# Half of the probability transposes of a cross-attention block move from TensorE to the DMA queue, and the weight scales' diagonal is made one step earlier

## The chip, the cores and the metric

The kernel runs on one core of a Trainium2 chip. A core has five engines that run side by side, each through its own instruction queue in order: TensorE (PE in the profile; its weight loads are listed apart as PEld), VectorE (DVE), ScalarE (ACT), GpSimd (POOL) and SyncE (SP), which here only issues DMA transfers. TensorE reads the on-chip memory SBUF and writes the accumulation memory PSUM, which GpSimd and the DMA engines do not touch in this kernel. Engines wait for one another through semaphores.

The metric is the device time of one execution in microseconds (us). Before the change the median of 3 runs is 666.36 us (665.87 to 667.03).

## The reference

Two blocks follow each other on x, which has 2 batches of 2048 tokens with 512 features (4096 tokens in all):

```
x = x + tanh(g_xattn) * (softmax(q k^T / sqrt(32)) v) Wo^T + ...   # q from layernorm(x); k, v from 77 context rows; 16 heads of 32
x = x + tanh(g_ffn)   * qlinear(gelu(qlinear(layernorm(x), w1, b1)), w2, b2)   # 512 -> 2048 -> 512
```

`qlinear` rounds its input and its weight to integers of at most 127 in size, with one scale per tensor: the largest absolute value over the whole tensor, divided by 127. So the scale of w1 and w2, of the normalized x, and of the hidden layer each need a maximum over everything before anything can be rounded. Attention is computed in 32-bit floats throughout.

## The kernel before

**Tiling.** The 4096 tokens are cut into 8 blocks of 512 (index i in the code, NB = 8), each of four tiles of 128 tokens (t = 0 to 3). The 16 heads are cut into 4 groups of 4 heads (g). One attention step s (0 to 7 in each block) is one group and one half of the block: g = s // 2, and two 128-token tiles, u = 0 and u = 1. There are 64 steps in all.

**One step of attention.** `softmax(i, s)` (L286 to L323) does, for 256 tokens and 4 heads: eight score matmuls into PSUM (L295), the maximum over the 77 keys on DVE (L304), the subtraction on DVE into the tile `e`, 128 partitions (tokens) by 2 x 4 x 77 (L308), the exponential on ACT (L314), the sum and its reciprocal on DVE (L316, L318), and the multiplication by the reciprocal on POOL (L319). `transpose_a(i, s, u)` (L325) turns the result round, since the product with V needs the keys on the partitions: four PE transposes of 128x77 into one PSUM tile `pt` (L332), and one ACT copy into `aT` (L333). It is called for u = 0 and u = 1 in each step. After both steps of a group, `apply_v(i, g)` (L335) makes four matmuls `pc` of V and `aT` (L341), which ACT copies to `cT` (L349).

**What else happens in a step.** The main loop (L455 to L517) weaves other work between: `project_q` (pq, L276), `project_o` of the block before (po, L354), transposes of the next block's normalized x (ptx, L267), layernorm statistics, and the maxima for the quantization of the second layernorm (`norm2_stats`, `norm2_max`, L365 to L382). The scores run two steps ahead: in step s, PE does `apply_v` of the group before (even s only), the scores of step s + 2, the transposes of step s, and then one pq or po. So the probabilities of step s have somewhat less than two steps to become ready for PE, and those of an odd step s are wanted by pc at the beginning of step s + 1.

**Weights.** In the same loop `weight_step` (L411) finds the maximum of w1 (block i = 1) and w2 (i = 3), turns them into scales at step 0 of i = 2 and i = 4 with `scale_of` (L166), and rounds the weights in i = 2 and i = 4 (`quantize`, L198). `scale_of` takes a maximum per partition (`m`), multiplies it onto the identity (`diag`, L172), and has PE multiply a matrix of ones with this diagonal (`pg`, L174), so that all 128 maxima stand on each partition, where DVE takes the final maximum (L176). Weights are loaded by SP in pieces of 1 MB into the same rotating buffers (`big`) that hold x; a load waits until its buffer is free.

**What sets the order.** The order on PE is that of the program text (`manual_schedule`). On the other engines, SP among them, a planner places each instruction by its own estimate of when its operands and its buffer are ready; `issue_after` adds that one instruction stays behind another on its engine. Once placed, an engine's order is fixed, and an instruction that waits holds all behind it.

**Afterwards.** The first product of the feed-forward part starts at about 429 us; it takes x transposed by DMA as 16-bit data (L584: `xqT` from `xq`, 128x512 each, 28 times), sends most hidden tiles to DRAM and brings them back for the second product. The change does not touch this part beyond the names of two helpers.

Of the kernel before, what the change touches and what calls it, by code (L numbers as in the profile page):

```python
# [7 lines left out]

F32 = mybir.dt.float32
BF16 = mybir.dt.bfloat16  # L10
AF = mybir.ActivationFunctionType
ALU = mybir.AluOpType
AX = mybir.AxisListType
# [2 lines left out]
P = 128  # L16
D = 512
KC = D // P
HEADS = 16
DK = D // HEADS  # L20
NK = 77
HG = P // DK
NG = HEADS // HG
# [19 lines left out]
def tile_flamingo_gated_block(  # L43
# [20 lines left out]
    nc = tc.nc  # L64
    B = ctxT.shape[0]
# [20 lines left out]
    def kchunks(w):  # L86
        return w.rearrange("(kc p) n -> p kc n", p=P)
# [4 lines left out]
    awts = actx.enter_context(tc.tile_pool(name="awts", bufs=1))  # L92
    wq_sb = awts.tile([P, KC, D], F32, name="wq_sb")
    wo_sb = awts.tile([P, KC, D], F32, name="wo_sb")
    ctx_sb = awts.tile([P, B, KC, NK], F32, name="ctx_sb")
    kblk = [awts.tile([P, NG, RK], F32, name=f"kb{b}") for b in range(B)]
    vblk = [awts.tile([NK, D], F32, name=f"vb{b}") for b in range(B)]
    work = actx.enter_context(tc.tile_pool(name="work", bufs=2))
    bv_sb = work.tile([NK, D], F32, tag="cT", name="bv_sb", bufs=7)
    bq_sb = const.tile([P, KC], F32, name="bq_sb")  # L100
    bk_sb = const.tile([P, KC], F32, name="bk_sb")
    tg = const.tile([P, 2], F32, name="tg")
# [7 lines left out]
        engine.dma_start(dst[:, :, c], kchunks(src)[:, :, c])  # L110

    def load_ctx(engine, b):
        engine.dma_start(ctx_sb[:, b, :, :], kchunks(ctxT[b]))

    load_x(0, pieces=NT, engines=(nc.sync, nc.scalar))
    load_ctx(nc.scalar, 0)
# [34 lines left out]
    xmax = const.tile([P, NB - 1 + NT], F32, name="xmax")  # L151
    hmax = const.tile([P, NB * GT * 2 + 1], F32, name="hmax")
# [10 lines left out]
        nc.gpsimd.tensor_tensor(rstd, ve, mhalf[:, :n], ALU.pow)  # L163
        return last

    def scale_of(maxima, name, psum, tag):  # L166


        m = const.tile([P, 1], F32, name=f"m_{name}")
        nc.vector.tensor_reduce(m, maxima, AX.X, ALU.max)  # L170
        diag = small.tile([P, P], F32, tag="diag", name=f"diag_{name}", bufs=1)
        nc.vector.tensor_scalar(diag, ident, m, None, ALU.mult)  # L172
        pg = psum.tile([P, 512], F32, tag=tag, name=f"pg_{name}")
        nc.tensor.matmul(pg[:, :P], ones, diag, start=True, stop=True)  # L174
        g = const.tile([P, 1], F32, name=f"g_{name}")
        nc.vector.tensor_reduce(g, pg[:, :P], AX.X, ALU.max)  # L176
        s = const.tile([P, 1], F32, name=f"s_{name}")
        nc.vector.tensor_scalar(s, g, MIN_RANGE, 1.0 / QP, ALU.max, ALU.mult)
        inv = const.tile([P, 1], F32, name=f"inv_{name}")
        nc.vector.reciprocal(inv, s)  # L180
        return s, inv
# [25 lines left out]
    with actx:  # L207
# [3 lines left out]

        for kb in kblk:
            nc.gpsimd.memset(kb, 0.0)

        def project_k(b, g):

            pk = ps_p.tile([P, 512], F32, tag="pp", name=f"pk{b}_{g}")
            for kc in range(KC):
                nc.tensor.matmul(  # L219
                    pk[:, :NK],  # L220
                    wk_sb[:, kc, g * P : (g + 1) * P],
                    ctx_sb[:, b, kc, :],
                    start=(kc == 0),
                    stop=(kc == KC - 1),
                )
            for j in range(HG):
                r = slice(j * DK, (j + 1) * DK)
                dst = kblk[b][r, g, j % RT * NK : (j % RT + 1) * NK]
                bias = bk_sb[r, g : g + 1]
                if j % 2 or b == 0:  # L230
                    nc.scalar.activation(dst, pk[r, :NK], AF.Identity, bias=bias)
                else:
                    nc.vector.tensor_scalar(dst, pk[r, :NK], bias, None, ALU.add)

        def project_v(b):

            pv = ps_p.tile([P, 512], F32, tag="pp", name=f"pvv{b}")
            for kc in range(KC):
                nc.tensor.matmul(  # L239
                    pv[:NK, :],  # L240
                    ctx_sb[:, b, kc, :],
                    wv_sb[:, kc, :],
                    start=(kc == 0),
                    stop=(kc == KC - 1),
                )
            nc.vector.tensor_tensor(vblk[b], pv[:NK, :], bv_sb, ALU.add)

        ln, xnT, qT, aT, cT, es = {}, {}, {}, {}, {}, {}

        def norm(i):  # L250

# [34 lines left out]
        def softmax(i, s):  # L286
            g, half = divmod(s, 2)
            n = f"{i}_{s}"

            ps = ps_s.tile([P, NR, 512], F32, tag="ps", name=f"ps{n}")  # L290
            for u in range(2):
                t = 2 * half + u
                for q in range(NR):
                    r = slice(q * RT * DK, (q + 1) * RT * DK)
                    nc.tensor.matmul(  # L295
                        ps[:, q, u * RK : (u + 1) * RK],
                        qT[i, g][r, t * P : (t + 1) * P],
                        kblk[i // NBB][r, g, :],
                        start=True,
                        stop=True,  # L300
                    )
            mx = small.tile([P, NR, 2, RT], F32, tag="mx", name=f"mx{n}")
            sc = ps[:, :, : 2 * RK].rearrange("p q (u r k) -> p q u r k", u=2, r=RT)
            nc.vector.tensor_reduce(mx, sc, AX.X, ALU.max)  # L304
            e = work.tile([P, 2, GK], F32, tag="e", name=f"e{n}", bufs=3)
            e4 = e.rearrange("p u (j k) -> p u j k", j=HG)
            last = {}
            last["DVE"] = nc.vector.tensor_tensor(  # L308
                e.rearrange("p u (q r k) -> p q u r k", q=NR, r=RT),
                sc,  # L310
                mx[:, :, :, :, None].to_broadcast([P, NR, 2, RT, NK]),
                ALU.subtract,
            ).ins
            last["ACT"] = nc.scalar.activation(e, e, AF.Exp, scale=SCALE).ins  # L314
            sm = small.tile([P, 2, HG], F32, tag="sm", name=f"sm{n}")
            nc.vector.tensor_reduce(sm, e4, AX.X, ALU.add)  # L316
            rs = small.tile([P, 2, HG], F32, tag="rs", name=f"rs{n}")
            nc.vector.reciprocal(rs, sm)  # L318
            last["POOL"] = nc.gpsimd.tensor_tensor(  # L319
                e4, e4, rs[:, :, :, None].to_broadcast([P, 2, HG, NK]), ALU.mult  # L320
            ).ins
            es[i, s] = e4
            return last  # L323

        def transpose_a(i, s, u):  # L325
            g, half = divmod(s, 2)
            t = 2 * half + u
            if t == 0:
                aT[i, g] = work.tile([NK, HG, TB], F32, tag="aT", name=f"aT{i}_{g}", bufs=3)
            pt = ps_t.tile([P, KC, P], F32, tag="pt", name=f"pta{i}_{s}_{u}")  # L330
            for j in range(HG):
                nc.tensor.transpose(pt[:NK, j, :], es[i, s][:, u, j, :], ident)  # L332
            nc.scalar.copy(aT[i, g][:, :, t * P : (t + 1) * P], pt[:NK, :, :])  # L333

        def apply_v(i, g):  # L335
            pc = ps_p.tile([P, TB], F32, tag="pp", name=f"pc{i}_{g}")
# [47 lines left out]

        wraw, wmax = {}, {}

        def load_w(name, src, pieces):
            for j in pieces:  # L390
                wraw[name, j] = big(f"raw_{name}{j}")
                nc.sync.dma_start(wraw[name, j], kchunks(src(j)))
# [18 lines left out]
        def weight_step(i, s):  # L411
            j, odd = divmod(s, 2)
            if i == 1 and odd:
                weight_max("w1", j)
            if i in (2, 4) and s == 0:
                name = "w1" if i == 2 else "w2"
                s_w[name], inv_w[name] = scale_of(wmax[name], name, ps_p, "pp")
            if i == 2 and odd:
                quantize(w1q[:, :, j * TB : (j + 1) * TB], wraw["w1", j], inv_w["w1"])
            if i == 3 and odd:  # L420
                weight_max("w2", j)
                if j < 2:
                    load_w("w2", w2_piece, [j + 2])
                else:
                    load_w("w2", w2_piece, [j - 2])
            if i == 4 and odd:
                quantize(w2q[:, j * KC : (j + 1) * KC, :], wraw["w2", j], inv_w["w2"])
                if j < 2:
                    load_w("w2", w2_piece, [j + 2])
# [22 lines left out]
        softmax(0, 0)  # L452
        softmax(0, 1)
        project_q(0, 1)
        for i in range(NB):  # L455
            for s in range(2 * NG):
                g, odd = divmod(s, 2)
# [10 lines left out]
                    last = softmax(i + 1, s + 2 - 2 * NG)  # L468
                for u in range(2):
                    transpose_a(i, s, u)  # L470
                if i == 0 and s == 1:
                    project_v(0)
                if i == 0 and s == 2:


# [51 lines left out]
                    last = norm2_max(NB - 1, t - 1, t)  # L527
        with tc.issue_after(last):
            norm2_max(NB - 1, NT - 1, NT)
        s_x, inv_x = scale_of(xmax, "x", ps_p, "pp")  # L530
        xq0 = work.tile([P, NT, D], BF16, tag="xnT", name="xq0", bufs=1)
        for t in range(NT):
            v, vq = xs0[:, t, :], xq0[:, t, :]
# [97 lines left out]
                    stored[i, a] = hidden_dram.tile([P, GF, TB], F32, name=f"h{i}_{a}")  # L631
                    nc.sync.dma_start(stored[i, a], G)
    w1ctx.close()
    s_h, inv_h = scale_of(hmax, "h", ps_g, "pg")
    s2 = const.tile([P, 1], F32, name="s2")


# [113 lines left out]
```

## Time and profile before

One execution was profiled. It took 665.6 us, of which 663.8 us are the span that the profile covers; the rest lies around it.

| | before |
|---|---|
| median of 3 runs | 666.36 us |
| profiled execution, its span | 665.6 us, 663.8 us |
| granted TensorE clock, mean | 0.979 |
| steady attention (i = 1 to 7) | 57.5 to about 404 us |
| end of attention to first feed-forward matmul | about 404 to 429 us |
| first product, second product | 429 to 546 us, 546 to 664 us |
| probability transposes on PE (pta) | 512, in 64 steps |
| ACT copies of them (aT) | 128, 68.3 us, 582 ns each |
| multiplications on POOL (e) | 64, 78.7 us, 1230 ns each |

In the page a group of instructions is written as line, engine, operation, output and inputs, shapes, count, then busy time and mean length of one, and at last the idle time of the engine before them and what ended it. A matmul's length contains the depth of the pipeline (285 ns for a transpose), so that what it takes from PE is read from the distance to the next one. A line of the waits names the waiting engine and line, who ended the wait, then total, number and longest in us. In a timeline a line gives start, length, engine, source line, operation and, in brackets, the idle time before and who ended it.

### The profile page before, as it was taken

To read this page: it belongs to the slowest core of one execution; us is meant where nothing else is said; L and a number is where in the kernel's file an instruction comes from. 1 tells how busy PE (TensorE), PEld (TensorE's weight loads), DVE (VectorE), ACT (ScalarE), POOL (GpSimd) and SP (SyncE) were. 2 spreads that over 40 slices of the span, in tenths; PEclk is the share of its full clock that TensorE was granted. 3 is DMA by queue.
4 is the path that set the end of the run, shared out by engine and by line. 5 is a ranking of instruction groups with operands and counts; after the bars stand their busy time and mean duration, and the time that the engine had idled before them with its cause. 6 is when DMAs were issued, how large, how long until landed. Compare 5 with 4: busy or idle time off the path is not lost.

```text
span 663.8 us, 8218 instructions
## 1 busy us (share of the span) xinstructions
PE 630.0 (95%) x3048; PEld 320.7 (48%) x3048; DVE 517.9 (78%) x809; ACT 342.9 (52%) x479; POOL 206.2 (31%) x161
## 2 busy tenths in 40 slices
PE   5999999899999899999999999599999979999997
PEld 4565555455455455455554554244444434444443
DVE  3676687887997997986876767999889878887441
ACT  4455444244444344444444442188999879645430
POOL 2234333243333243333333332000000009996000
PEclk9999999799999899999999999799999998999999
DMA  9902100023131113100000000079999208789962
GB/s 280 377 22 88 39 1 0 1 70 121 64 120 72 64 71 120 64 0 1 1 0 1 1 17 1 0 255 329 303 309 345 77 0 326 274 324 357 335 206 79
DMA packets 44255, 84.90 MB, mean 128 GB/s; under 512 B 18795, under 2 KB 22891, under 8 KB 38584
## 3 DMA queue, kind: packets, MB, share of 16 engines
q1 hardware_dynamic: 43112, 83.70, 35.8%
q10 hardware_dynamic: 1104, 0.69, 0.3%
q8 instruction: 24, 0.39, 0.2%
q14 instruction: 15, 0.12, 0.1%
HBM read 49.25 MB, written 31.46 MB: 122 GB/s over the span
## 4 chain that ended last, share of the span: by engine, by line
PE 87%; DVE 10%; ACT 2%; DMA 1%; issue 1%; POOL 0%; ACTq 0%; DVEq 0%
PE pf L668 17%; PE ph L604 17%; PE po L354 15%; PE pq L276 14%; PE pta L332 9%; PE ps L295 6%; PE pc L341 4%; PE ptx L267 2%; DVE tm L376 1%; DVE xf L185 1%; DVE e L308 1%; PE pvv L239 1%; PE pk L219 1%; DVE mx L304 1%; DVE sm L316 1%; DVE max_w L397 1%
## 5 line engine op out<-in xcount | busy, mean ns | idle before, releaser
L319 POOL TENSOR_TENSOR e<-e,rs 128x616 f32<-128x616 f32 x64 | 78.7, 1230 | 231.2 <-DVE rs L318 173.4
L276 PE MATMUL pq<-xnT,wq_sb 128*128 128x512 f32 x256 | 117.3, 602 | 0.8 <-ACT xnT L268 0.8
L668 PE MATMUL pf<-w2q,hq 128*128 128x512 bf16 x512 | 113.6, 386 | 2.3 <-DVE hq L201 2.0
L354 PE MATMUL po<-wo_sb,cT 128*128 128x512 f32 x256 | 114.8, 593 | 0.0
L604 PE MATMUL ph<-xqT,w1q 128*128 128x512 bf16 x512 | 112.1, 382 | 0.7 <-DVE xqT L544 0.7
L333 ACT COPY aT<-pta 77x512 f32<-77x512 f32 x128 | 68.3, 582 | 77.0 <-PE pta L332 76.9
L611 ACT ACTIVATE G<-ph,b1s,s 128x512 f32<-128x512 f32 x128 | 99.5, 778 | 14.1 <-PE ph L604 3.3
L314 ACT ACTIVATE e<-e 128x616 f32<-128x616 f32 x64 | 45.9, 717 | 75.0 <-DVE e L308 73.4
L668 PEld LDWEIGHTS <-hq 128*128 128x128 bf16 x512 | 50.7, 99 | 64.9 <-issue 3.6
L621 DVE TENSOR_REDUCE hmax<-G 128x1 f32<-128x1024 f32 (+1 forms) x65 | 76.6, 1196 | 6.7 <-ACT G L611 6.7
L604 PEld LDWEIGHTS <-w1q 128*128 128x128 bf16 x512 | 50.3, 99 | 62.2 <-issue 1.9
L332 PE MATMUL pta<-ident,e 128*77 128x128 f32 x512 | 72.0, 285 | 0.1
L304 DVE TENSOR_REDUCE mx<-ps 128x8 f32<-128x616 f32 x64 | 50.3, 786 | 27.9 <-PE ps L295 27.4
L276 PEld LDWEIGHTS pq<-xnT,wq_sb 128*128 128x128 f32 x256 | 47.2, 194 | 48.7 <-issue 47.8
L316 DVE TENSOR_REDUCE sm<-e 128x8 f32<-128x616 f32 x64 | 50.6, 790 | 24.7 <-ACT e L314 24.5
L354 PEld LDWEIGHTS po<-wo_sb,cT 128*128 128x128 f32 x256 | 46.4, 190 | 48.2 <-issue 46.6
L332 PEld LDWEIGHTS pta<-ident,e 128*77 128x77 f32 x512 | 57.1, 150 | 11.8 <-issue 10.4
L661 ACT ACTIVATE Gb<-Gb,inv_h 128x2048 f32<-128x2048 f32 x22 | 43.7, 2000 | 36.5 <-DMA Gb<-h 35.5
L295 PEld LDWEIGHTS ps<-kb,qT 64*128 64x128 f32 x512 | 36.4, 188 | 44.9 <-ACT qT L284 22.8
L682 POOL TENSOR_TENSOR x<-x,b_sb 128x512 f32<-128x512 f32 x32 | 56.2, 1793 | 0.1
L308 DVE TENSOR_TENSOR e<-ps,mx 128x616 f32<-128x616 f32 x64 | 51.0, 797 | 2.6
L295 PE MATMUL ps<-kb,qT 64*128 64x154 f32 x512 | 51.3, 320 | 1.6 <-ACT qT L284 1.5
(89 smaller groups left out, 594.7 us busy)
## 6 DMA issues: line engine op xcount, KB each, us to landing
h<-G SPq DMA_DIRECT2D x22, 1024.0 KB, 5.7
Gb<-h SPq DMA_DIRECT2D x22, 1024.0 KB, 7.5
raw_w<-in_w2T SPq DMA_DIRECT2D x8, 1024.0 KB, 5.0
out_y<-x SPq DMA_DIRECT2D x32, 256.0 KB, 2.8
x<-in_x SPq DMA_DIRECT2D x7, 1024.0 KB, 5.3
raw_w<-in_w1T SPq DMA_DIRECT2D x4, 1024.0 KB, 11.7
wk_sb<-in_wkT SPq DMA_DIRECT2D x4, 256.0 KB, 4.9
wq_sb<-in_wqT SPq DMA_DIRECT2D x4, 256.0 KB, 6.1
```

The lines of the kernel that those rows point to most:

```text
L276: nc.tensor.matmul(pq, wq_sb[:, kc, g * P : (g + 1) * P], xnT[i][:, kc, :], start=(kc == 0), stop=(kc == KC - 1),)
L295: nc.tensor.matmul(ps[:, q, u * RK : (u + 1) * RK], qT[i, g][r, t * P : (t + 1) * P], kblk[i // NBB][r, g, :], start=True, stop=True,)
L308: last["DVE"] = nc.vector.tensor_tensor(e.rearrange("p u (q r k) -> p q u r k", q=NR, r=RT), sc, mx[:, :, :, :, None].to_broadcast([P, NR, ...
L316: nc.vector.tensor_reduce(sm, e4, AX.X, ALU.add)
L319: last["POOL"] = nc.gpsimd.tensor_tensor(e4, e4, rs[:, :, :, None].to_broadcast([P, 2, HG, NK]), ALU.mult).ins
L332: nc.tensor.transpose(pt[:NK, j, :], es[i, s][:, u, j, :], ident)
L333: nc.scalar.copy(aT[i, g][:, :, t * P : (t + 1) * P], pt[:NK, :, :])
L354: nc.tensor.matmul(po, cT[i, g][:, t * P : (t + 1) * P], wo_sb[:, g, :], start=(g == 0), stop=(g == NG - 1),)
L604: nc.tensor.matmul(ph, w1q[:, kc, fc * P : (fc + 1) * P], cur[:, kc, :], start=(kc == 0), stop=(kc == KC - 1),)
L611: nc.scalar.activation(G[:, 2 * v + u, :], ph, AF.Gelu, bias=b1s[:, fc : fc + 1], scale=s1,)
L621: nc.vector.tensor_reduce(hmax[:, k + u : k + u + 1], G[:, 2 * v + u : 2 * v + u + n, :], AX.XY, ALU.max, apply_absolute_value=True,)
L668: nc.tensor.matmul(po[t], hq[:, fc, t * P : (t + 1) * P], w2q[:, fc, :], start=(fc == 0), stop=(fc == FC - 1),)
```

## The change

For each step the second tile (u = 1) takes another way. After the multiplication on POOL, a second POOL instruction reads the 4 x 77 floats of each token as pairs of 16-bit words and writes low and high halves apart into a buffer `planes`, 128 x (2 halves x 4 heads x 128), of which two exist, used in turn and zeroed once. A DMA on SP's queue transposes each of its eight 128x128 blocks into `eT` (two buffers). `transpose_a` for u = 1 is then one ACT copy that reads both halves from `eT` and interleaves them again into floats in `aT`. For u = 0 nothing changes.

To make room, the context `ctx_sb` no longer has its own storage: its two batches take two of the seven slots of `cT`, which are not yet in use then. `project_v(0)` is moved from step 1 of the first block to ahead of the loop.

`scale_of` is cut in two: `diagonal_of` (maximum per partition, diagonal) and the rest. For w1 and w2 the diagonal is made at step 7 of i = 1 and 3, and the matmul stays at step 0 of i = 2 and 4. For x and the hidden layer both halves are still called together.

```diff
-    ctx_sb = awts.tile([P, B, KC, NK], F32, name="ctx_sb")
+    ctx_sb = [work.tile([P, KC, NK], F32, tag="cT", name=f"ctx{b}", bufs=7) for b in range(B)]
+    planes = [awts.tile([P, 2, HG, P], U16, name=f"planes{k}") for k in range(2)]
...
-    def scale_of(maxima, name, psum, tag):
+    def diagonal_of(maxima, name):
         m = const.tile([P, 1], F32, name=f"m_{name}")
         nc.vector.tensor_reduce(m, maxima, AX.X, ALU.max)
         diag = small.tile([P, P], F32, tag="diag", name=f"diag_{name}", bufs=1)
         nc.vector.tensor_scalar(diag, ident, m, None, ALU.mult)
+        return diag
+
+    def scale_of(diag, name, psum, tag):
         pg = psum.tile([P, 512], F32, tag=tag, name=f"pg_{name}")
         nc.tensor.matmul(pg[:, :P], ones, diag, start=True, stop=True)
...
         for kb in kblk:
             nc.gpsimd.memset(kb, 0.0)
+        for half in planes:
+            nc.gpsimd.memset(half, 0)
...
             es[i, s] = e4
+            p = planes[s % 2]
+            words = e4[:, 1, :, :].bitcast(U16).rearrange("p j (k h) -> p h j k", h=2)
+            nc.gpsimd.tensor_copy(p[:, :, :, :NK], words)
+            eT[i, s] = work.tile([P, 2, HG, P], U16, tag="eT", name=f"eT{n}", bufs=2)
+            nc.sync.dma_start_transpose(
+                eT[i, s].rearrange("p h j n -> p (h j) n"), p.rearrange("p h j k -> p (h j k)")
+            )
             return last
...
-            pt = ps_t.tile([P, KC, P], F32, tag="pt", name=f"pta{i}_{s}_{u}")
+            dst = aT[i, g][:, :, t * P : (t + 1) * P]
+            if u == 1:
+                nc.scalar.copy(
+                    dst.bitcast(U16).rearrange("p j (n h) -> p h j n", h=2), eT[i, s][:NK]
+                )
+                return
+            pt = ps_t.tile([P, KC, P], F32, tag="pt", name=f"pta{i}_{s}")
             for j in range(HG):
                 nc.tensor.transpose(pt[:NK, j, :], es[i, s][:, u, j, :], ident)
-            nc.scalar.copy(aT[i, g][:, :, t * P : (t + 1) * P], pt[:NK, :, :])
+            nc.scalar.copy(dst, pt[:NK, :, :])
...
             if i in (2, 4) and s == 0:
                 name = "w1" if i == 2 else "w2"
-                s_w[name], inv_w[name] = scale_of(wmax[name], name, ps_p, "pp")
+                s_w[name], inv_w[name] = scale_of(wdiag[name], name, ps_p, "pp")
...
+            if i in (1, 3) and s == 2 * NG - 1:
+                name = "w1" if i == 1 else "w2"
+                wdiag[name] = diagonal_of(wmax[name], name)
...
         project_q(0, 1)
+        project_v(0)
...
-                if i == 0 and s == 1:
-                    project_v(0)
```

More of the change, by code (lines that the diff above doesn't have):

```diff
@@ L10 @@
 BF16 = mybir.dt.bfloat16
+U16 = mybir.dt.uint16
 AF = mybir.ActivationFunctionType
@@ L112, in load_ctx @@
     def load_ctx(engine, b):
-        engine.dma_start(ctx_sb[:, b, :, :], kchunks(ctxT[b]))
+        engine.dma_start(ctx_sb[b], kchunks(ctxT[b]))
     load_x(0, pieces=NT, engines=(nc.sync, nc.scalar))
@@ L221, in project_k @@
                     wk_sb[:, kc, g * P : (g + 1) * P],
-                    ctx_sb[:, b, kc, :],
+                    ctx_sb[b][:, kc, :],
                     start=(kc == 0),
@@ L240, in project_v @@
                     pv[:NK, :],
-                    ctx_sb[:, b, kc, :],
+                    ctx_sb[b][:, kc, :],
                     wv_sb[:, kc, :],
@@ L246, in project_v @@
             nc.vector.tensor_tensor(vblk[b], pv[:NK, :], bv_sb, ALU.add)
-        ln, xnT, qT, aT, cT, es = {}, {}, {}, {}, {}, {}
+        ln, xnT, qT, aT, cT, es, eT = {}, {}, {}, {}, {}, {}, {}
         def norm(i):
@@ L382, in norm2_max @@
             ).ins
-        wraw, wmax = {}, {}
+        wraw, wmax, wdiag = {}, {}, {}
         def load_w(name, src, pieces):
@@ L529, in tile_flamingo_gated_block @@
             norm2_max(NB - 1, NT - 1, NT)
-        s_x, inv_x = scale_of(xmax, "x", ps_p, "pp")
+        s_x, inv_x = scale_of(diagonal_of(xmax, "x"), "x", ps_p, "pp")
         xq0 = work.tile([P, NT, D], BF16, tag="xnT", name="xq0", bufs=1)
@@ L633, in tile_flamingo_gated_block @@
     w1ctx.close()
-    s_h, inv_h = scale_of(hmax, "h", ps_g, "pg")
+    s_h, inv_h = scale_of(diagonal_of(hmax, "h"), "h", ps_g, "pg")
     s2 = const.tile([P, 1], F32, name="s2")
```

## The prediction

> **What bounds the kernel now.** I read the page's first part, then windows cut at the first score matmul of each 512-token block, then the waits, then a timeline of single steps. Columns of a window: length, busy time and instruction count of PE, PEld, DVE, ACT, POOL, then granted clock, DMA share, GB/s.
>
> ```profile
> PE 630.0 (95%) x3048; PEld 320.7 (48%) x3048; DVE 517.9 (78%) x809; ACT 342.9 (52%) x479; POOL 206.2 (31%) x161
> ...
> 57.50:105.60 48.10, 48.10 (x252) 25.73 (x248) 36.39 (x61) 22.34 (x39) 16.30 (x15) 1.00 0.13 44
> 105.60:159.50 53.90, 50.87 (x248) 27.51 (x244) 46.20 (x79) 21.39 (x36) 18.35 (x14) 0.94 0.12 40
> 159.50:206.80 47.30, 47.26 (x244) 25.14 (x240) 43.00 (x74) 20.85 (x36) 17.77 (x15) 1.00 0.24 90
> 206.80:259.20 52.40, 49.37 (x248) 26.65 (x244) 46.19 (x79) 21.39 (x36) 18.62 (x14) 0.97 0.21 81
> 259.20:306.50 47.30, 47.26 (x244) 25.15 (x240) 38.28 (x71) 21.06 (x36) 18.95 (x15) 1.00 0.13 45
> 306.50:353.80 47.30, 47.30 (x246) 25.22 (x242) 35.81 (x67) 21.09 (x36) 16.76 (x14) 1.00 0.00 1
> ```
>
> These are i = 1 to 6. Attention is bound by PE with no gap, except in i = 2 and i = 4, and DVE is close behind: 46.2 us of work in i = 2 and 4, 43.0 in i = 3. The exceptions are one wait each:
>
> ```profile
> PE pg_w L174 <- DVE rs L318: 6.1, 2, 3.0
> ...
> 122.30:125.30 3.00, 0.00 (x0) 0.03 (x1) 2.91 (x8) 0.72 (x1) 0.00 (x0) 0.95 0.01 3
> 125.30:134.00 8.70, 8.70 (x30) 5.13 (x30) 6.82 (x15) 1.78 (x3) 3.65 (x3) 0.63 0.00 0
> ```
>
> PE stands 3.0 us for the weight maximum's diagonal, then runs at clock 0.63: the two steps concerned span 18.0 us (117.0 to 135.0) where an ordinary pair takes 11.4. Excess 6.6 us in i = 2, and likewise 16.5 against 11.4, 5.1 us, in i = 4.
>
> The distance that the DMA route must fit in is seen in one odd step:
>
> ```profile
> 206.77 1.22 POOL L319 TENSOR_TENSOR e<-e,rs 128x616 f32<-128x616 f32 x1 [3.84 <-ACT qT L284]
> ...
> 212.72 0.87 PEld L332 LDWEIGHTS pta<-ident,e 128*77 128x77 f32 x8 [0.16 <-POOL e L319]
> ...
> 213.66 3.60 PE L276 MATMUL pq<-xnT,wq_sb 128*128 128x512 f32 x8
> ...
> 217.19 1.06 PE L341 MATMUL pc<-aT,vb 77*32 77x512 f32 x8
> ```
>
> The probabilities multiplied at 206.77 are ready at 207.99, PE transposes them at 212.72 (eight in 0.94 us, up to pq), and the product with V needs them at 217.19. From "ready" to pc is 9.2 us here. Over all odd steps of i = 1 to 6 I find 7.9 to 15.0 us, mostly 8.4 to 11; even steps have one step (over 5 us) more. The last step of all has only 2.8 us.
>
> [...] no one-input copy is in this trace, and the two-input multiply of 616 elements takes 1217 ns[...].
>
> **The change, part by part.**
>
> *PE transposes.* 4 of 8 leave each of 64 steps: half of 0.94 less the start, 0.45 us. 64 x 0.45 = 28.8 us at most, 3.6 per block.
>
> *Diagonal earlier.* m_w and diag_w (0.14 + 0.28 us of DVE) move one step ahead of the pg matmul, some 5 us. DVE is behind at that place (norm-2 maxima of the block before), but the diagonal now stands before the next scores, not behind them. PE's wait and slow clock should go: 6.6 and 5.1 us as far as PE is concerned. But then DVE bounds those blocks.
>
> *Blocks.* After = the larger of (PE without the excess, less 3.6) and (DVE work, plus about 1.8 us of waits for exp that DVE cannot fill, 5.7 us over i = 2 to 4). i = 1: 44.5 (-3.6). i = 2: PE 43.7, DVE 46.2 + 1.8 = 48.0 (-5.9). i = 3: DVE 43.0 + 1.8 = 44.8 (-2.5). i = 4: DVE 48.0 (-4.4). i = 5, 6, 7: PE (-3.6 each). i = 0: -3.0, since the first loads occupy the DMA engines until about 33 us, and the first two transposes queue behind them; project_v(0) moved forward fills PE's 1.3 us idle at 24.5. Sum -30.2.
>
> *Separation on GpSimd.* [...] POOL rises from 18 to 26 us of 44 per block: not a bound. Behind the copy stand the add of bo and rstd; the copy also waits for the plane's transpose of two steps before, long done. A busier POOL may slow DVE's tensor_scalar work (xf took 0.53 alone and 0.80 beside a multiply): inside my losses below.
>
> *DMA transpose.* The page's row:
>
> ```profile
> xqT<-xq SPq DMA_TRANSPOSE x28, 3.7
> ```
>
> That is four 128 x 128 blocks each: 1.19 us of SP and 2.4 us to landing when nothing else moves, 3.7 median beside stores, 6.5 at most. The new one has eight blocks. I add 1.2 us for the four more: SP 2.4, landing 3.6 to 3.7 (bounds 2.6, if the cost is all fixed, and 7.4, twice the median). Per block of 44 us SP issues 8 x 2.4 = 19 us, the DMA engines are busy about 8 x 1.2: neither binds.
>
> *Joining on ACT.* Two 77x512 copies at 582 ns become one and a 1024-element copy. ACT rows of 616 and 2048 elements (717 and 2000 ns) give 0.9 ns per element and 165 fixed: 1.08 us[...]. ACT goes from 21 to 25 us per block. Not a bound, but the join waits for a DMA with exp, qT and cT queued behind it.
>
> *Chain.* Copy 1.1, SP and landing 3.8, join 1.2: 6.1 us after "ready". Available at odd steps: the 8.4 to 11 above less three half transposes, 1.35, so 7 to 9.6; the tightest is 7.9 - 1.35 = 6.6. It just fits, everywhere but at the end: the last step has 2.8 - 0.4 = 2.4, so PE stands 3.7 us before the last pc, with nothing to cover it, and perhaps a slow clock after: **+3.9**.
>
> *Loads on the same queue.* From 60 us on 14 loads of 1 MB share SP's ring, each occupying the engines about 3 us. A transpose issued behind one comes 2 to 3 us late; at odd steps 1 of these is slack. 14 x 0.7 (chance to be hit) x 0.5 (odd) x 1.3 is about **+6**. SP is in order too: a load waiting for its buffer (up to 71.8 us for x, on w1q) would stop the transposes behind it. The planner places a load when its buffer falls free by its own estimate, so a mismatch of 1 to 2 us per load is what I expect; with ACT's joins standing a little before exp I put **+4** (0 to 15) for both.
>
> Moving ctx_sb to the cT slots and two memsets on an idle POOL: nothing.
>
> Sum: -30.2 + 3.9 + 6 + 4 = -16.3. The profiled execution (665.6 us, span 663.8) goes to about 649; the median shown is 0.8 above that execution, so **650 us**.
>
> **Rivals.**
>
> *The DMA route is too long (slower).* From the score matmul to pc PE has about 15.2 us of work left per odd step (two short steps of 4.7, one long of 5.7), and the chain takes 7.5 (to "ready") + 1.1 + landing + 1.3. If landing is D, every pair of steps stalls by half of D - 5.3, because the stall before also counts. At D = 7.4 that is 1.05 us x 30 pairs, 31 us, in place of the +6: 675. It turns from gain to loss near D = 6.5. For it: 6.5 has been seen, with half the size. Against: those stood beside 1 MB stores, and attention moves 1 to 90 GB/s.
>
> *ACT stands in joins (slower).* If the planner reckons a shorter DMA than the chip's, each join holds exp and DVE starves. In i = 2 to 4 DVE has no room, so each us per step costs 24; at 1 us per step 650 + 24 = 674, deciding from 0.7 us. For it: ACT is in order and the planner doesn't know real landings. Against: exp has slack against its next use elsewhere.
>
> *All hides (faster).* The loads and joins cost nothing: -26, so 640; with DVE's work spread over neighbouring blocks 636.
>
> *The change does nothing:* excluded by PE's lost work, unless stalls eat it; I count 3 in 100 for landing within 0.2%, about what measurement can tell from no change.
>
> **How the numbers follow.** Likeliest 0.56 (own range 641 to 661), all hides 0.12, DMA too long 0.16, ACT in joins 0.16, of which the two slower ones end under the old time 3 times in 100 and within 0.2% 3 times. Faster 0.71, same 0.03, slower 0.26. The range takes in the rivals' centres: 637 to 677.
>
> **What would show it.** Right: no wait of pg on DVE; half the pta count; blocks of 44 to 45 us with PE full in i = 1, 5, 6, DVE near full in i = 2 to 4; transposes landing in 3 to 5 us; a gap of 3 to 5 us before the last pc. Wrong: pc waiting for ACT aT in most pairs (DMA too long), ACT's idle put down to the DMA with DVE waiting for exp (joins), SP waiting for a load's buffer while probabilities lie ready, or a separation copy over 2 us.

## The result, and the profile after

The changed kernel is slower. Its median is 719.89 us (718.20 to 721.02, 4 runs) beside 666.12 us (664.34 to 667.03, 4 runs) for the kernel before: a ratio of 1.0813, 95% interval 1.0783 to 1.0844. The prediction was 650 us. The profiled execution took 718.2 us with a span of 716.4 us, 52.6 us longer than the span before.

First the page's part on engines, then its groups of instructions; both of the kernel after. Its line numbers differ a little from those of before: the score matmul `ps` is L303, the exponential L322, the multiplication on POOL L327, the separation L335, the DMA transpose L337, the join L349, the remaining copy behind PE's transposes L356, the product `pc` L364.

```profile
PE 627.1 (88%) x2792; PEld 303.4 (42%) x2792; DVE 520.8 (73%) x809; ACT 385.1 (54%) x479; POOL 257.1 (36%) x227
...
L349 ACT COPY aT<-eT 77x1024 uint16<-77x1024 uint16 x64 | 85.6, 1338 | 108.3 <-DMA eT<-planes 108.3
...
L335 POOL COPY planes<-e 128x616 uint16<-128x616 uint16 x64 | 51.6, 806 | 2.0
```

PE has 256 instructions fewer and fell from 95% to 88% of the span. The group that stands out is the join: each takes 1338 ns, and ahead of the 64 of them ACT stood idle for 108.3 us in all, until the landing of a DMA.

Windows of the kernel after, cut at the first score matmul of each block, i = 1 to 6 (length, then busy time and count of PE, PEld, DVE, ACT, POOL, granted clock, DMA share, GB/s):

```profile
64.30:116.60 52.30, 46.97 (x222) 23.39 (x218) 36.49 (x61) 28.27 (x42) 22.48 (x22) 0.97 0.35 81
116.60:171.20 54.60, 44.64 (x212) 21.98 (x212) 46.60 (x79) 26.54 (x37) 26.20 (x22) 0.98 0.38 90
171.20:226.20 55.00, 48.29 (x210) 23.91 (x210) 44.26 (x72) 26.50 (x37) 23.52 (x22) 0.93 0.46 115
226.20:282.50 56.30, 47.87 (x212) 23.68 (x212) 46.59 (x79) 26.67 (x37) 26.19 (x22) 0.93 0.42 113
282.50:337.60 55.10, 48.93 (x208) 23.84 (x208) 38.26 (x69) 26.25 (x37) 23.14 (x22) 0.91 0.28 63
337.60:393.20 55.60, 49.36 (x208) 24.76 (x208) 36.41 (x67) 26.40 (x37) 21.73 (x22) 0.88 0.20 38
```

No engine fills its block: in i = 5 and 6 PE is busy 49 of 55 us, and part of that is its slower clock (0.91 and 0.88, 1.00 before). Before, these blocks took 47.3 us with PE full. The weights' blocks i = 2 and 4 no longer stand out; all blocks from i = 2 on take 54.6 to 59.0 us. So the loss is spread over all blocks: the eight grew by about 49 us together, from 0.8 us in i = 2, where the earlier diagonal gains, to 9.7 in i = 7. What lies between them and the first feed-forward product grew by 3.4.

The waits of the kernel after (engine and line, who ended the wait, total, number, longest):

```profile
ACT aT L349 <- DMA eT<-planes: 108.3, 53, 5.4
PEld ps L303 <- ACT qT L292: 56.2, 24, 6.1
DVE sm L324 <- ACT e L322: 54.2, 33, 4.6
PE ps L303 <- ACT qT L292: 34.6, 17, 5.2
PEld pc L364 <- ACT aT L349: 9.2, 2, 5.9
PE pc L364 <- ACT aT L349: 8.2, 2, 5.6
```

Three of these were far smaller before:

```profile
DVE sm L316 <- ACT e L314: 24.5, 35, 0.8
PEld ps L295 <- ACT qT L284: 22.8, 25, 2.2
PE ps L295 <- ACT qT L284: 1.5, 2, 1.3
```

The product that uses the joined data waits only twice, for 8.2 us. What waits is unrelated to it: DVE's sum for an exponential, and PE's scores for queries. Both are made on ACT, where they can stand behind a join. A timeline of the kernel after shows one such case (start, length, engine, line, operation, and in brackets the idle time before and who ended it; lines of other work left out):

```profile
309.72 0.70 POOL L335 COPY planes<-e 128x616 uint16<-128x616 uint16 x1
...
311.53 0.79 DVE L316 TENSOR_TENSOR e<-ps,mx 128x616 f32<-128x616 f32 x1
...
313.56 1.34 ACT L349 COPY aT<-eT 77x1024 uint16<-77x1024 uint16 x1 [3.68 <-DMA eT<-planes]
314.77 0.70 ACT L322 ACTIVATE e<-e 128x616 f32<-128x616 f32 x1
...
315.51 0.80 DVE L324 TENSOR_REDUCE sm<-e 128x8 f32<-128x616 f32 x1 [1.14 <-ACT e L322]
...
318.25 1.07 PE L364 MATMUL pc<-aT,vb 77*32 77x512 f32 x8
...
319.21 0.72 ACT L322 ACTIVATE e<-e 128x616 f32<-128x616 f32 x1 [1.97 <-DVE mean L162]
...
319.84 0.67 ACT L292 ACTIVATE qT<-pq,bq_sb 128x512 f32<-128x512 f32 x1
...
320.56 0.80 PE L303 MATMUL ps<-kb,qT 64*128 64x154 f32 x8 [1.24 <-ACT qT L292]
```

DVE has the scores of two steps on subtracted at 312.32. ACT could take their exponential then, but the join is ahead of it in ACT's order and waits for its transfer until 313.56. The exponential starts at 314.77, 2.45 us late, while the product that needs this join runs only at 318.25. The delay runs on from there: DVE stands 1.14 us for this exponential, so its next subtraction ends only at 319.10 (not shown) and the next exponential starts at 319.21. Behind that one, in ACT's order, stands the copy of queries whose projection was done at about 317.45 (not shown); it starts at 319.84, and PE's scores that read it start after 1.24 us of idling. In the whole kernel PE idles 34.6 us for queries, 1.5 before. ACT kept its order here: the exponential's operand was ready at 312.32, and nothing passed the join that waited until 313.56.

### The profile page after: what moved, and what is told of

It reads as the page before. It is cut to its first block, busy times and chain, and to the rows that moved or that the text cites. A ratio compares the mean times of both kernels' runs of the same rounds, so it can differ in the third digit from the quotient of the medians.

```text
span 716.4 us, 8015 instructions
## 1 busy us (share of the span) xinstructions
PE 627.1 (88%) x2792; PEld 303.4 (42%) x2792; DVE 520.8 (73%) x809; ACT 385.1 (54%) x479; POOL 257.1 (36%) x227
## 3 DMA queue, kind: packets, MB, share of 16 engines
q1 hardware_dynamic: 110696, 100.48, 47.2%
## 4 chain that ended last, share of the span: by engine, by line
PE 46%; DVE 22%; DMA 12%; POOL 7%; ACT 6%; issue 6%; SPq 0%; POOLq 0%; DVEq 0%; ACTq 0%
PE pf L693 16%; PE ph L629 16%; DMA eT<-planes 11%; PE po L377 8%; DVE sm L324 3%; POOL planes L335 3%; DVE e L316 3%; DVE mx L312 3%; ACT aT L349 2%; POOL x L279 2%; ACT e L322 2%; PE ps L303 2%; DVE x L384 2%; DVE xf L191 2%; POOL e L327 2%
## 5 line engine op out<-in xcount | busy, mean ns | idle before, releaser
L327 POOL TENSOR_TENSOR e<-e,rs 128x616 f32<-128x616 f32 x64 | 78.7, 1230 | 237.2 <-DVE rs L326 149.3
L349 ACT COPY aT<-eT 77x1024 uint16<-77x1024 uint16 x64 | 85.6, 1338 | 108.3 <-DMA eT<-planes 108.3
L377 PE MATMUL po<-wo_sb,cT 128*128 128x512 f32 x256 | 127.4, 646 | 0.0
L303 PE MATMUL ps<-kb,qT 64*128 64x154 f32 x512 | 55.7, 341 | 34.7 <-ACT qT L292 34.6
L377 PEld LDWEIGHTS po<-wo_sb,cT 128*128 128x128 f32 x256 | 52.1, 214 | 56.8 <-issue 54.9
L303 PEld LDWEIGHTS ps<-kb,qT 64*128 64x128 f32 x512 | 39.8, 203 | 79.7 <-ACT qT L292 56.2
L322 ACT ACTIVATE e<-e 128x616 f32<-128x616 f32 x64 | 45.7, 714 | 47.8 <-DVE e L316 39.2
L284 PEld LDWEIGHTS pq<-xnT,wq_sb 128*128 128x128 f32 x256 | 47.2, 195 | 48.8 <-issue 47.7
L686 ACT ACTIVATE Gb<-Gb,inv_h 128x2048 f32<-128x2048 f32 x22 | 43.7, 2000 | 33.9 <-DMA Gb<-h 33.9
L356 ACT COPY aT<-pta 77x512 f32<-77x512 f32 x64 | 36.9, 577 | 46.5 <-PE pta L355 46.4
L335 POOL COPY planes<-e 128x616 uint16<-128x616 uint16 x64 | 51.6, 806 | 2.0
```

The lines of the kernel that those rows point to most:

```text
L284: nc.tensor.matmul(pq, wq_sb[:, kc, g * P : (g + 1) * P], xnT[i][:, kc, :], start=(kc == 0), stop=(kc == KC - 1),)
L303: nc.tensor.matmul(ps[:, q, u * RK : (u + 1) * RK], qT[i, g][r, t * P : (t + 1) * P], kblk[i // NBB][r, g, :], start=True, stop=True,)
L327: last["POOL"] = nc.gpsimd.tensor_tensor(e4, e4, rs[:, :, :, None].to_broadcast([P, 2, HG, NK]), ALU.mult).ins
L335: nc.gpsimd.tensor_copy(p[:, :, :, :NK], words)
L349: nc.scalar.copy(dst.bitcast(U16).rearrange("p j (n h) -> p h j n", h=2), eT[i, s][:NK])
L377: nc.tensor.matmul(po, cT[i, g][:, t * P : (t + 1) * P], wo_sb[:, g, :], start=(g == 0), stop=(g == NG - 1),)
```

## The experiments

**Theory A** (from the profile above): the loss is the wait for a DMA in ACT's order. The route itself is cheap and early enough for `pc`; but the planner set every join ahead of the exponential of two steps on, and some directly ahead of a query copy, so the DMA's latency enters the chain that feeds the next scores. **Rivals**: the extra work itself (longer join, separation copy, DMA traffic); the transfer too late for `pc`; the changed place of the diagonal. The first four kernels tell these apart.

**The join without the wait.** It does the same work on constants, so the second tile's probabilities are left out of the result.

```diff
             if u == 1:
+                halves = ones[:NK].bitcast(U16).rearrange("p (h n) -> p h n", h=2)
+                halves = halves[:, :, None, :].to_broadcast([NK, 2, HG, P])
                 nc.scalar.copy(
-                    dst.bitcast(U16).rearrange("p j (n h) -> p h j n", h=2), eT[i, s][:NK]
+                    dst.bitcast(U16).rearrange("p j (n h) -> p h j n", h=2), halves
```

> The join is kept on ACT with its size and place in the step, but it reads a constant tile of ones in place of the transposed halves, so that it waits for no DMA (the second tile's probabilities are then not the true ones). Separation and DMA transposes still run. Theory A (ACT stands in joins that the planner put ahead of exp and qT, waiting for the DMA): all of the loss and most of the hoped gain come back, 645 to 660 us, and the waits of DVE for exp and of PE for qT shrink to the old size. Theory B (POOL, SP and DMA work in itself slows DVE or delays the probabilities, whoever reads them): stays above 700. Theory C (the join's length, 1.34 us in place of 0.58, overloads ACT): stays above 690.

Measured: 648.24 us (one run), span 646.5. All instructions are there, the joins keep their length and their places ahead of the exponentials, and 71.6 us are gone. Of the difference in span, 69.9 us, PE's busy time is 23.0 (627.1 against 604.1 for the same work, at a mean granted clock of 0.942 against 0.976) and its idle time 46.9. The joins of this kernel, and two of its waits:

```profile
L351 ACT COPY aT<-ones 77x1024 uint16<-77x1024 uint16 x64 | 83.5, 1337 | 0.1
...
DVE sm L324 <- ACT e L322: 27.0, 27, 1.7
PE ps L303 <- ACT qT L292: 4.9, 4, 1.7
```

**The join behind the exponential of two steps on.**

```diff
-                for u in range(2):
-                    transpose_a(i, s, u)
+                transpose_a(i, s, 0)
+                with tc.issue_after(last["ACT"]):
+                    transpose_a(i, s, 1)
```

> Only the order on ACT changes: each join is tied behind the exponential of the scores made in the same step; data, DMA and waits are those of the change. Theory A (order on ACT): exp is no longer held, DVE's wait for exp falls from 54 to about 25 us, and the time comes down to 650 to 680. Theory B2 (the chain from separation to join is too long for the two steps there are, whatever the order): stays at 705 to 725, with the wait moved to pc for aT.

Measured: 673.82 us (667.93 to 675.92, 4 runs), ratio to before 1.0101 (1.0052 to 1.0151). The order alone takes 46 us off the changed kernel, with the real transfer in place. It also moves the wait, as these waits of this kernel show:

```profile
PEld pc L364 <- ACT aT L349: 40.2, 22, 4.8
DVE sm L324 <- ACT e L322: 24.4, 29, 1.4
PE pc L364 <- ACT aT L349: 22.9, 18, 4.0
...
ACT aT L349 <- DMA eT<-planes: 9.5, 6, 2.9
```

ACT hardly waits any more and DVE's waits are those of before; now PE waits for late joins.

**The extra work without its use.** PE's transposes and both ACT copies stay; separation, DMA and the earlier diagonal are added, and nothing reads `eT`.

```diff
-            if u == 1:
-                nc.scalar.copy(
-                    dst.bitcast(U16).rearrange("p j (n h) -> p h j n", h=2), eT[i, s][:NK]
-                )
-                return
```

> All eight PE transposes and both ACT copies of before are kept, and separation on POOL and the DMA transpose run beside them with nobody reading the result; the diagonal is early as in the change. Theory A: the side work costs nearly nothing, 655 to 668 us (the early diagonal gains up to 10). Theory B (side work itself): 690 or more, near the changed kernel.

**The earlier diagonal alone**, on the kernel before, with `scale_of` cut in two as in the change (not shown):

```diff
+            if i in (1, 3) and s == 2 * NG - 1:
+                name = "w1" if i == 1 else "w2"
+                wdiag[name] = diagonal_of(wmax[name], name)
```

> The kernel before with only the diagonal of w1 and w2 a step earlier. My prediction's term: PE's two waits of 3.0 us and the slow clock after them go, 6 to 11 us, so 655 to 661 us. A rival: DVE is behind at that place anyway and PE waits for it at the next scores, 664 to 667.

Measured: 658.83 us with the side work (one run), and 656.79 us with the diagonal alone (656.34 to 656.94, 4 runs; ratio 0.9874, 0.9858 to 0.9889). The diagonal is worth 8.3 us (i = 2 fell from 53.8 to 48.4 us, i = 4 from 52.4 to 48.4), and all the side work costs about 2. Together with the kernel above, which has the longer joins, this puts the rivals of extra work and of the diagonal out.

**The wait alone.** This adds to the side-work kernel one ACT copy of a single column of `eT` per step. Nothing uses it, and the planner places it.

```diff
+            if u == 1:
+                peek = small.tile([NK, 1], U16, tag="peek", name=f"peek{i}_{s}")
+                nc.scalar.copy(peek, eT[i, s][:NK, 0, 0, :1])
```

> The side-work kernel (all PE transposes and both ACT copies as before, separation and DMA beside them, early diagonal; 658.8 us) plus one ACT copy of a single column of the transposed halves per step, placed by the planner. It adds no length to speak of (64 copies of some 0.2 us, 13 us of an engine half idle) and nobody uses it: all that it adds is ACT's wait for the DMA. Theory A: the wait alone brings most of the loss back, 690 to 725. If the wait is harmless: 659 to 664.

Measured: 706.57 us (701.71 to 709.53, 4 runs), ratio 1.0635 (1.0601 to 1.0668). Its group and its waits:

```profile
L354 ACT COPY peek<-eT 77x1 uint16<-77x1 uint16 x64 | 12.4, 194 | 145.4 <-DMA eT<-planes 145.3
```

```profile
DVE sm L324 <- ACT e L322: 63.4, 41, 4.1
PEld ps L303 <- ACT qT L292: 45.5, 26, 4.2
```

Copies that are busy for 12.4 us together cost 48 us, with the same two victims as in the changed kernel. No product depends on them. That settles theory A's core: the wait in the order is enough for a loss of this size. What makes up the rest of the 71.6 was not separated.

**The join on GpSimd** (`nc.scalar.copy` becomes `nc.gpsimd.tensor_copy`):

> The join runs on POOL in place of ACT, with the order left to the planner; the rest as in the change. Theory A (what counts is who stands behind the waiting join): on POOL there stand the next multiply, which needs 5 us anyway, so that the waits of DVE for exp and of PE for qT go back to the old size and the time falls to 655 to 680. Theory B2 (chain too long): stays near 700 to 720, with pc waiting for aT.

Measured: 721.03 us (720.41 to 723.78, 4 runs), ratio 1.0842 (1.0814 to 1.0870). This kernel's waits:

```profile
POOL aT L349 <- DMA eT<-planes: 109.3, 46, 4.6
PEld pc L364 <- POOL aT L349: 35.2, 15, 6.3
```

The time expected under theory A (655 to 680) was missed. DVE's waits for exponentials did fall to their old size (22.0 us), but the same wait now stands on the engine that also holds the next multiplication: PE idled 23.3 us for late joins and 10.6 for late probabilities. Taking the join off ACT freed ACT and helped nothing. By itself this kernel would fit the rival of a transfer too late for `pc` as well.

**Repairs that missed.** Five kernels tried to give the route more time. In "separate first", the separation copy must come ahead of the bias additions on POOL:

```diff
-            nc.gpsimd.tensor_copy(p[:, :, :, :NK], words)
+            last["POOL"] = nc.gpsimd.tensor_copy(p[:, :, :, :NK], words).ins
```

> The addition of bo on POOL is tied behind the separation copy (in the change it often stands between multiply and copy, 1.27 us); all else as in the change. Theory A (joins stand ahead of exp and qT on ACT and wait there): the DMA is up to 1.3 us earlier where the addition stood in between, about half of the steps, so ACT's wait for the DMA falls by 20 to 40 us and the time by 10 to 30, to 690 to 710. Theory B2 (chain too long): about the same number. It sizes this part of the chain.

In "product later", `pc` of groups 0 to 2 moves from the start of the even step into the odd step after it, ahead of the query projection, some 5 us later:

```diff
-                if not odd and s > 0:
-                    apply_v(i, g - 1)
-                elif not odd and i > 0:
+                if not odd and s == 0 and i > 0:
                     apply_v(i - 1, NG - 1)
...
+                if odd and s > 1:
+                    apply_v(i, g - 1)
```

> The product with V of groups 0 to 2 moves from the beginning of the even step to the odd step after it, some 5 us later in PE's order; the order on ACT is left to the planner. Theory A: pc was not what stood, exp and qT behind the joins were, so little is won: 705 to 720. Theory B2 (the chain is too long for the time up to pc): the slack cures it, 650 to 670.

With the planner's order of ACT, these measured 712.73 and 716.03 us (one run each): a few us, with ACT's wait still 98.8 and 111.8. The first fell short of what was expected. The second was expected at 650 to 670 if the transfer were too late for `pc`, so that rival is out as the cause. Both together, and the join behind the exponential:

> Three edits together: the product with V later, the join behind the exponential of its step, separation ahead of the addition of bo. Theory A says that the 25 us still missing between the join behind exp (673.8) and the join without a wait (648.2) are pc waiting for a join that now comes late; with 5 us more up to pc most of it should come back: 648 to 660, and pc's wait for aT falls from 40 to under 15 us. If it stays at 670 or more, the rest is something else (SP, buffers of eT).

Measured: 682.40 us (681.00 to 684.36, 4 runs), ratio 1.0258 (1.0228 to 1.0289), worse than the late join alone and far from the 648 to 660 expected. Two more hold both joins of a group back until the odd step's query copy has been issued; the second also covers group 3, for which the output projection `po` is split so that `pc` comes behind three quarters of it:

```diff
+                if odd and held_back:
+                    with tc.issue_after(behind):
+                        transpose_a(i, s - 1, 1)
+                        transpose_a(i, s, 1)
```

> For head groups 0 to 2 of a block, the product with V stands one step later on PE, and both joins of the group are tied on ACT behind qT of the odd step, so that neither exp nor qT can stand behind a join that waits; the joins of group 3 are left to the planner. Theory A: three quarters of the excess over the join without a wait go, 655 to 668. If the loss came from the chain's length or from SP or the buffers eT (which are now held longer): 675 or more.

> As the kernel with joins behind qT, and group 3 too: its product with V stands behind three quarters of the po of step 0, whose last quarter moves to step 1. Theory A: ACT never waits for a transpose in steady state, 645 to 656, as fast as the join without a wait, and the fastest correct version. If something else in the route costs: 660 or more.

Measured: 681.33 us (one run) and 681.15 us (677.85 to 683.73, 4 runs; ratio 1.0235, 1.0195 to 1.0274); both missed what was expected. In the second ACT waits only 3.2 us for the DMA, and yet it stays 33 us above the kernel without the wait. What PE waited for there was queries, `PEld ps <- ACT qT` 36.3 us (23.7 in the kernel without the wait). So a second loss had come in with the rewrite. The next two kernels look for it.

**The product later, with no DMA at all**, on the kernel with the earlier diagonal (same edit as above):

> The kernel before with the earlier diagonals (656.8 us), all transposes on TensorE, and the products with the values of groups 0 to 2 moved from the start of the even step into the odd step ahead of the query projection. Theory U (uncovered queries): what the last three rewrites lost is the product's cover over the query's copy: the scores that read it now come 0.8 to 1.1 us too late in 24 of 32 pairs of steps. This kernel has no DMA and no join, so it loses the same 20 to 30 us: 677 to 687 us, with over 40 us of TensorE's waits for queries instead of 23. Theory J (joins): the loss in those rewrites is the joins' time on ScalarE, and moving the product by itself costs next to nothing: 656 to 661 us.

Measured: 673.02 us (one run), 16.2 above its base. Its timeline, PE alone:

```profile
254.67 1.06 PE L345 MATMUL pc<-aT,vb 77*32 77x512 f32 x8
255.67 3.70 PE L280 MATMUL pq<-xnT,wq_sb 128*128 128x512 f32 x8
260.14 0.80 PE L299 MATMUL ps<-kb,qT 64*128 64x154 f32 x8 [0.78 <-ACT qT L288]
```

In the original order `pc` (1 us) stands between the query projection and the scores that read its result, and covers ACT's copy of the queries. Moved ahead of the projection, it leaves PE idle 0.78 us here; in the whole kernel PE idles 13.0 us for queries, 1.5 in its base. The loss, 16 us, is below the 20 to 30 expected: it explains about half of the 33. The other half is not settled; PE's transposes also waited for normalized x behind two joins there (14.5 us), which was seen but not tested.

**The route in the middle blocks alone**, i = 1 to 6, joins behind the exponential:

```diff
+        def by_dma(i, s):
+            return 0 < i < NB - 1
```

> The joins behind the exponentials (673.8 us), with the DMA route in blocks 1 to 6 alone and TensorE's transposes in the first and last block. Theory E (edges): against the kernel without the wait, the joins behind the exponentials lose 8.8 us in block 0 and 9.1 us in block 7, so without the route there some 15 us come back, less 5 us that TensorE transposes longer: 660 to 665 us. Theory M (middle too): TensorE still waits for late joins of odd steps inside the six blocks, and the edges only showed what any block loses: 668 to 676 us.

Measured: 659.06 us (657.95 to 662.27, 4 runs), ratio 0.9917 (0.9890 to 0.9944). Without the route in the first and last block the late join's 673.82 falls by 14.8, a little more than expected; PE's waits for joins fell to 25.4 (loads) and 11.5 us. This is 0.8% faster than before, but slower than the diagonal alone.

**The route in even steps alone**, where `pc` comes a whole step later; i = 1 to 7, joins behind the exponential, PE's transposes elsewhere (27 of 64 steps):

```diff
+            return 0 < i and s % 2 == 0 and not (i == NB - 1 and s == 6)
```

> The changed kernel with the DMA route in 27 of its 64 steps alone: the even steps of blocks 1 to 7 without the last; everywhere else TensorE transposes as before. The joins stand behind the exponentials of two steps on. An even step's product runs a whole step later than an odd step's, so a join issued some 2 us later is still early there. Theory A (what costs is that something stands in ScalarE's or TensorE's order behind a transfer that has not landed): with the waits gone the 27 saved groups of transposes (0.45 us each, 12 us) show, less 2 us of side work and up to 3 us of longer joins: 645 to 652 us, the fastest of the kernels that compute the reference. Rival (the route costs more than it saves wherever it is put, through the joins' 1.34 us on ScalarE and the copies on GpSimd): 657 to 665 us, no faster than with the earlier diagonals alone.

Measured: 654.18 us (651.77 to 655.53, 5 runs), ratio 0.9841 (0.9822 to 0.9860). PE's waits now list none for a late join, but the time lies above the 645 to 652 expected, and the gain over the diagonal alone is only 2.6 us. Blocks 2 and 4 took 49.6 us, longer than the 48.4 with PE's transposes, with DVE busy for 46.0 and 46.1 of them (44.4 there). The last kernel leaves out these two:

```diff
-            return 0 < i and s % 2 == 0 and not (i == NB - 1 and s == 6)
+            return i in (1, 3, 5, 6, 7) and s % 2 == 0 and (i, s) != (7, 6)
```

> The route in even steps (654.2 us) without blocks 2 and 4, so in 19 steps. Those two blocks took 49.6 us each with the route and 48.5 with TensorE's transposes in the kernel with the earlier diagonals, though TensorE was busy 1.7 us less: VectorE sets their length there, with the maximum over a weight (46.0 of 49.6 us busy). If that reading holds, each goes back to 48.5 and the rest stays: 652 us (651 to 653.5). If the lengths of single blocks are chance of one execution, the 8 saved groups of transposes are lost instead: 656 to 658 us.

Measured: **648.98 us** (648.58 to 649.51, 5 runs), ratio to before 0.9757 (0.9743 to 0.9770). Blocks 2 and 4 took 48.0 us each, and the others kept their lengths within 0.4 us. The time lies below the expected range, which started from the median of 654.18; the two profiled executions (651.77 and 648.98 us) differ by 2.8, the two blocks by 3.1. It is the fastest version that computes the whole result, faster than both kernels: 16.5 us under the 665.51 measured beside it, and 7.8 under the diagonal alone. Not all of that is the route's. In the profiles, whose spans differ by 7.1, 5.4 us lie in the five blocks that have the route, where 19 saved groups of transposes are worth at most 19 x 0.45 = 8.6; 0.9 lie in blocks 2 and 4 and 0.6 ahead of block 1, without the route. Its joins and, below, ACT's timeline in one stretch:

```profile
L354 ACT COPY aT<-eT 77x1024 uint16<-77x1024 uint16 x19 | 25.1, 1324 | 0.1
```

```profile
265.08 0.72 ACT L325 ACTIVATE e<-e 128x616 f32<-128x616 f32 x1 [4.96 <-DVE e L319]
265.70 1.31 ACT L354 COPY aT<-eT 77x1024 uint16<-77x1024 uint16 x1
```

ACT's idle time ahead of the joins is 0.1 us in all, where it was 108.3: each stands behind an exponential, and its transfer has landed by then.

## Why the prediction was wrong

**The step that failed** is the term "+4 (0 to 15)" for ACT's joins "standing a little before exp" together with SP's order. All its terms for waiting came to 13.9 us (+3.9, +6 and +4); the waits measured 71.6 with their consequences (719.9 against 648.2 without them), 46 of which the joins' place before the exponential alone decides, and a wait with nothing else attached measured 48. So of the 70 us between forecast and result, 58 lie in the waits and 12 in the blocks' sum below. Mechanism and place had been named, as the rival "ACT stands in joins" with a chance of 0.16, but it too was mis-sized, at 674. The prediction priced late joins only in i = 2 to 4, where DVE is full, and set aside the other blocks because "exp has slack against its next use elsewhere". The windows show the opposite: i = 5 and 6, where DVE is busy only 38 and 36 us, became as long as the others. A slack of one engine did not help, since the exponential stands in the same queue as the queries' copy, whose lateness PE feels directly: in i = 5 and 6 PE waited 6.8 and 7.9 us for queries, most of its idle time. How much of it came through a late exponential, and how much from a join directly ahead of the copy, was not separated. Nor did the term count PE's clock: 23 of the 69.9 us are PE working slower, at a granted clock of 0.942 against 0.976 without the wait.

**The deadline that was checked was the wrong one.** "It just fits" compared the chain of 6.1 us with the time until `pc`. In the changed kernel `pc` hardly waits for a join, but its blocks of 55 us also gave it more time than was reckoned; whether the chain would have fitted at the forecast pace is not shown. The join had two deadlines: its consumer's, and that of what stood behind it in ACT's queue. In the timeline above the join was wanted by `pc` at 318.25, but held up an exponential from 312.32 on: the second was 6 us tighter.

**The sizes of the route** held or came out smaller, but for the join. The landing was put at 3.6 to 3.7 us and measured 3.1 (3.0 to 6.5); SP's issue at 2.4 and measured 1.23; the separation, put at 1.1 in the chain (the author's estimate, with no copy of its kind in the trace), measured 0.81 in the mean; the join, put at 1.08, took 1.34 us. The rival "DMA route too long" is out as the cause here, though late joins do make PE wait once they stand where they delay nobody else: behind the exponential, 40.2 us of PE's weight loads waited for them.

**PE's saving and the diagonal.** The diagonal's wait fell from 6.1 to 1.1 us and its effect was 8.3 us; 5.9 + 4.4 had been put for both blocks, including the transposes. The sum of the blocks, -30.2, was too large. Without any wait for the DMA the prediction's terms leave about 636, and 648.2 was measured: blocks 3, 5 and 7 took 47.2, 47.2 and 48.4 us there instead of 44.8, 43.7 and 45.7. So its closeness to 650 is luck and confirms nothing. Why these blocks saved so little stays open; PE was busy in them for 45.6, 45.5 and 45.1 us, at a granted clock of 0.96, and idle for the rest. In the version with 19 steps, 5.4 us in the blocks concerned are 0.28 us per step, not 0.45.

**The end.** The +3.9 was low: the last `pc` waited 5.6 us, and the `po` behind it took 16.6 us instead of 14.0, at a mean granted clock of 0.84 over these 16.6 us (0.50 in the first 3.9) against 1.00 before: the slow clock that had been named as possible.

**SP's order.** The transposes waited on POOL's separation (227.7 us in 51 waits), not on a load's buffer; beside that, SP's waits ahead of them show 0.7 us for a load and 7.4 us for `eT`'s own buffers. The +6 for landings behind loads was not measured by itself.

## What to carry to other kernels

When a transfer's result is consumed on an engine that has other work queued behind the consumer (here ACT, idle for 108.3 us ahead of the joins), place that instruction where its transfer has surely landed, by an explicit order, and choose the work whose own consumer comes late enough for it: here the kernel with 19 steps on the DMA is 7.8 us under the earlier diagonal alone, and the one with all 64 in the planner's order 63 above it. Before pricing an offload, list what stands behind the first waiting instruction and who needs that next. And moving an instruction away from a place gives up what it covered there: products of 1 us each, moved to the next step in three of four head groups, cost 16 us in all without any DMA.

## What the runs showed of the hardware

SP's issue of one transpose instruction took 1.23 us in the median with eight blocks of 128x128 (kernel after), and with four blocks (kernel before) 1.19 us at the least and 1.22 to 1.30 for the four that stood alone: between these two sizes the issue did not grow with the blocks. Landing rose only from 2.4 to 2.6 us (four blocks, nothing else moving) to 3.1 us in the median. The 1024-element 16-bit interleaving copy took 1.34 us on ACT, and GpSimd's separation of 616 16-bit elements 0.70 us in the median. In the kernel before, `xf` on DVE took 1.14 us where it began beside a multiplication on POOL (at 118.1 us), and the next one 0.53 us with POOL idle; the prediction's 0.80 is half of the 1.60 that the two took together.
